# A graph transformer on one core: one token tile is attended without a rank, before the others

## Chip, cores, metric

One Trainium2 chip, one NeuronCore. The metric is the device time of one execution in microseconds (us). Engines are called PE (TensorE), DVE or VectorE, ACT (ScalarE), POOL (GpSimd) and SP (SyncE).

## The reference

Two layers of a graph transformer over N = 2708 tokens of width 512, with 8 heads of 64 and a hidden width of 2048, all in fp32. Each layer computes, with its own weights:

```python
mask = adj + eye(n)
q, k, v = (h @ W.T + b for W, b in ((Wq, bq), (Wk, bk), (Wv, bv)))     # 8 heads of 64
scores = where(mask == 0, -1e9, q k^T / 8)
ctx = softmax(scores) @ v
h1 = layer_norm(h + ctx @ Wo.T + bo)
h2 = layer_norm(h1 + relu(h1 @ W1.T + b1) @ W2.T + b2)
```

`adj` is a symmetric 2708 x 2708 integer matrix with about 9 ones in a row (at most 20), so a token attends to few others.

## The kernel before

Tokens are handled in tiles of 128; there are 22 tiles, and the last one, number 21, has 20 tokens.

**Lists.** While the keys and values of layer 0 are projected (22 tiles, `kv_d` in memory), each row of `adj` is read and VectorE takes from it the list of neighbours, up to 24 entries in `top` (`lists`). Then `counted` counts each row's neighbours and sums them by length. `ranked` turns that into a rank for each token, sorted by length with the longest first. It writes each token's record (its list and its own number) into the table `rec_d` at its rank, with 22 indirect DMAs from POOL, one for each tile, and loads the table back as `new`. From then on "tile g" means the 128 tokens with ranks 128 g and on. `listed` makes from `new` the gather indices `idx` and the mask terms `minus`; `ident_i` holds each rank's token.

**Slots.** `CAPS[g]` says how many neighbours the longest list of tile g may have: 22 for tile 0 down to 3 for tile 21, 210 in all. Attention of a tile gathers one key and value row for each token in each slot (`gather`, one indirect DMA of 128 rows of 4 KB for each slot), two slots to a chunk. For a chunk VectorE multiplies by the query (L1055) and reduces (L1061), ACT takes the exponentials (L1074) and weighs the second slot (L1081), VectorE weighs the first (L1087) and adds (L1094). At a tile's end `sums` and `divided` give its context `cx`. The first chunk may only be issued when `idx` of that tile exists; `kv` has five buffers.

**Order.** The kernel runs over 11 blocks of two tiles, in the order `blocks = [(20, 19), (18, 17), (7, 9), ...]`. In each block PE turns the two contexts (`flip`, L1191), projects them (`o`), VectorE normalises, and PE runs the feed-forward network in 16 steps f, `pf` (L1383) and `a` (L1356), with ACT's ReLU (`ft`, L1394) between them. Attention of later blocks is a generator; `advance(credit)` issues as many of its steps as the credit pays (a full chunk costs 1), and `through(k)` issues what block k still lacks, at f = 10 of the block before. At most two finished contexts wait at a time. The order of PE, ACT and SP is the program's; that of POOL and VectorE is too in the stage in question (`manual_schedule`), and elsewhere a scheduler sets it.

**Layer 0's queries.** After the keys come 22 queries (`first_queries`), tiles in order, from a second reading of x in blocks of 256 columns (`xg`), written to `q_d` at the tokens' own places. At t = 1 `ranked` is issued. At t = 12 (`OWN` − 1) the first lists are used. The first four rank tiles do not wait for `q_d`: their x rows are gathered (`own_rows`), turned and projected once more (`own_query`). Near the end of this stage block (20, 19) is attended and its contexts are projected.

**Layer 1** reuses ranks, lists and the same block order.

## Time and profile before

| | |
|---|---|
| median of 3 runs | 1948.09 us (1946.08 to 1949.13) |
| the profiled execution | 1944.02 us, span 1942.3 us |
| mean granted PE clock | 0.982 |
| keys of layer 0 | 0 to 157 us |
| queries of layer 0 and the first block's attention | 157 to 290 us |
| layer 0's blocks | 290 to 1145 us |
| change of layers | 1145 to 1235 us |
| layer 1's blocks | 1235 to 1942 us |

Engine times in the profile are busy times; a PE that is busy can still run at half the clock, which the granted clock shows. In a timeline, the bracket behind a row gives how long the engine stood idle before it and what released it. "Issue" means that no wait is seen.

### The profile page before, as it was taken

How to read it: one execution, taken by the hardware profiler on the slowest of the kernel's cores; microseconds unless marked ns; L12 is line 12 of the kernel's file. 1: busy time of each engine (PE TensorE's matmuls, PEld its weight loads, DVE VectorE, ACT ScalarE, POOL GpSimd, SP SyncE). 2: the span in 40 equal slices, each digit the busy share in tenths (PEclk: the TensorE clock that was granted, in tenths of full speed). 3: DMA queues.
4: the chain of work that ended last, by engine and by line, in shares of the span. 5: the costliest groups of instructions: out<-in, count | busy, mean ns of one | idle time of the engine just before them, and what ended most of it. 6: DMA issues, size and time to landing. Idle time of an engine off the chain costs nothing.

```text
span 1942.3 us, 20878 instructions
## 1 busy us (share of the span) xinstructions
PE 1859.4 (96%) x6162; PEld 1098.8 (57%) x6162; DVE 1321.4 (68%) x2172; ACT 934.0 (48%) x3219; POOL 804.6 (41%) x710
## 2 busy tenths in 40 slices
PE   8998968999999999999999997999999999999997
PEld 4443426556666565665666553566666665666664
DVE  5885467758658686785840337697977998878422
ACT  4560135545536555474452113556465766655511
POOL 3013525435536555463510114354555776546101
PEclk9999978999999999999999999999999999999999
DMA  9998747556645665554501368665665766544000
GB/s 330 345 319 297 260 151 269 181 176 198 199 159 181 215 201 175 188 185 151 170 17 65 110 237 325 215 220 186 216 213 165 262 215 235 184 154 151 17 1 19
DMA packets 131486, 366.92 MB, mean 189 GB/s; under 512 B 16669, under 2 KB 37005, under 8 KB 128655
## 3 DMA queue, kind: packets, MB, share of 16 engines
q0 software_dynamic: 69120, 246.35, 38.0%
q1 hardware_dynamic: 53332, 99.66, 14.9%
q10 hardware_dynamic: 8910, 19.48, 2.7%
q8 instruction: 50, 0.82, 0.2%
q14 instruction: 74, 0.60, 0.1%
HBM read 314.62 MB, written 50.83 MB: 188 GB/s over the span
## 4 chain that ended last, share of the span: by engine, by line
PE 48%; issue 3%; DVE 3%; DMA 1%; POOL 1%; ACT 1%; POOLq 0%; SPq 0%; DVEq 0%
PE pf L1383 19%; PE a L1356 18%; PE o L576 4%; PE q L576 2%; PE k L576 1%; PE v L576 1%; PE tp L1191 1%; DVE kv L1055 1%; POOL kv L1018 1%; DVE sc L1061 1%; DMA kv<-kv_d,idx 1%; PE a L1371 1%; DMA q<-q_d 0%; DVE acc L1094 0%; POOL rd L1181 0%
## 5 line engine op out<-in xcount | busy, mean ns | idle before, releaser
L1018 POOL DMA_INDIRECT kv<-kv_d,idx x420 | 544.5, 1296 | 461.8 <-DVE acc L1094 272.4
L1383 PE MATMUL pf<-hT,w 128*128 128x256 f32 (+1 forms) x2816 | 637.2, 374 | 6.7 <-ACT ft L1394 5.2
L1383 PEld LDWEIGHTS pf<-hT,w 128*128 128x128 f32 x2816 | 521.4, 192 | 181.8 <-issue 104.1
L1356 PE MATMUL a<-w,ft 128*128 128x512 f32 x1312 | 615.0, 595 | 6.1 <-ACT ft L1394 3.6
L1055 DVE TENSOR_TENSOR kv<-kv,q 128x1024 f32<-128x1024 f32 (+3 forms) x222 | 254.3, 1157 | 171.1 <-DMA kv<-kv_d,idx 139.9
L1394 ACT ACTIVATE ft<-pf,b 128x256 f32<-128x256 f32 (+1 forms) x336 | 153.8, 463 | 432.7 <-PE pf L1383 428.8
L1356 PEld LDWEIGHTS a<-w,ft 128*128 128x128 f32 x1312 | 247.8, 191 | 196.5 <-issue 169.3
L1081 ACT ACTIVATE kv<-kv,p 128x64 f32<-128x64 f32 x1232 | 311.0, 334 | 5.0
L1061 DVE TENSOR_REDUCE sc<-kv 128x16 f32<-128x1024 f32 (+3 forms) x222 | 253.7, 1152 | 1.5
L1094 DVE TENSOR_TENSOR acc<-acc,kv 128x1024 f32<-128x1024 f32 (+2 forms) x178 | 203.9, 1145 | 17.5 <-ACT kv L1081 15.5
L1181 POOL TENSOR_TENSOR rd<-va,mhalf 128x1 f32<-128x1 f32 (+1 forms) x88 | 90.0, 1023 | 273.5 <-DVE va L1179 271.9
L576 PE MATMUL o<-wo,cT 128*128 128x512 f32 x336 | 149.7, 598 | 0.5 <-ACT cT L1196 0.5
L1087 DVE TENSOR_TENSOR kv<-kv,p 128x512 f32<-128x512 f32 (+1 forms) x178 | 121.2, 681 | 36.1 <-ACT p L1074 36.1
L1074 ACT ACTIVATE p<-sc,minus 128x8 f32<-128x8 f32 x420 | 102.8, 294 | 72.0 <-DVE sc L1061 43.6
L1125 ACT ACTIVATE cx<-acc,su 128x64 f32<-128x64 f32 (+1 forms) x352 | 88.5, 334 | 71.1 <-DVE su L1117 54.2
L576 PEld LDWEIGHTS o<-wo,cT 128*128 128x128 f32 x336 | 64.1, 192 | 82.3 <-issue 72.1
L681 ACT ACTIVATE code<-aj 128x2708 bf16<-128x2708 int32 (+1 forms) x22 | 73.2, 3328 | 50.2 <-POOL aj L677 41.7
L684 DVE MAX8 tops<-code 128x8 f32<-128x247 f32 (+2 forms) x242 | 83.1, 401 | 20.1 <-ACT code L681 20.1
L1185 DVE SCALAR_TENSOR_TENSOR h<-h,rd,ln_b 128x512 f32<-128x512 f32 (+1 forms) x88 | 65.6, 746 | 41.1 <-POOL rd L1181 41.1
L1081 ACT ACTIVATE acc<-kv,p 128x64 f32<-128x64 f32 (+1 forms) x352 | 88.8, 335 | 1.4
L1443 ACT COPY kvs<-v 128x512 f32<-128x512 f32 (+1 forms) x22 | 12.9, 585 | 158.8 <-PE v L576 138.4
L1415 DVE TENSOR_TENSOR h<-a,h 128x512 f32<-128x512 f32 (+1 forms) x44 | 29.8, 678 | 83.3 <-PE a L1356 44.5
(159 smaller groups left out, 1586.8 us busy)
## 6 DMA issues: line engine op xcount, KB each, us to landing
aj<-in_adj SPq DMA_DIRECT2D x21, 1354.0 KB
kv_d<-kvs ACTq DMA_DIRECT2D x21, 512.0 KB
w<-in_W SPq DMA_DIRECT2D x20, 512.0 KB
xg<-in_xT SPq DMA_DIRECT2D x19, 512.0 KB
kv<-kv_d,idx POOLq DMA_INDIRECT x420
w<-in_W ACTq DMA_DIRECT2D x12, 512.0 KB
q_d<-qs SPq DMA_DIRECT2D x22, 256.0 KB
zT_d<-zT SPq DMA_DIRECT2D x22, 256.0 KB
```

The source lines that it names most:

```text
L576: nc.tensor.matmul(o[:r], xs(c), wm[:, c, :], start=(c == 0), stop=(c == NC - 1))
L1018: return nc.gpsimd.indirect_dma_start(out=to, out_offset=None, in_=table[:, :], in_offset=bass.IndirectOffsetOnAxis(ap=s, axis=0), bounds_ ...
L1055: nc.vector.tensor_tensor(kv[:r, :c, :DM], kv[:r, :c, :DM], self.q[:r].unsqueeze(1).to_broadcast([r, c, DM]), ALU.mult,)
L1061: nc.vector.tensor_reduce(self.sc[:r, s0 : s0 + c, :], kv[:r, :c, :DM].rearrange("p s (h d) -> p s h d", d=DK), AX.X, ALU.add,)
L1074: nc.scalar.activation(p[:r, s, :], self.sc[:r, s, :], AF.Exp, bias=minus[:r, g, s : s + 1])
L1081: nc.scalar.activation(to[:, i, hd], kv[:r, i, DM + h * DK : DM + (h + 1) * DK], AF.Copy, scale=p[:r, s0 + i, h : h + 1],)
L1087: nc.vector.tensor_tensor(to[:, 0, :].rearrange("p (h d) -> p h d", d=DK), kv[:r, 0, DM:].rearrange("p (h d) -> p h d", d=DK), p[:r, s0, : ...
L1094: nc.vector.tensor_tensor(self.acc[:r, :c, :], self.acc[:r, :c, :], kv[:r, :c, DM:], ALU.add)
L1181: nc.gpsimd.tensor_tensor(rd[:r], va[:r], mhalf[:r], ALU.pow)
L1356: nc.tensor.matmul(a[:r], fts[f][:, c0 : c0 + r], self.w2[f // 2][:, f % 2, :], start=(f == 0), stop=(f == NFC - 1),)
L1383: nc.tensor.matmul(pf[:, :w], self.w1[f // 2][:, c, f % 2 * P : f % 2 * P + P], hT[:, c, :w], start=(c == 0), stop=(c == NC - 1),)
L1394: nc.scalar.activation(ft[:, :w], pf[:, :w], AF.Relu, bias=self.b1[:, f : f + 1])
```

## The change

Tile 18 in token order (tokens 2304 to 2431, `STAR`) is taken out of the ranking. It keeps its tokens' own order and becomes place 20 (`FRESH`), with a cap of 18; the other tokens share the other places, and those whose rank falls behind place 20 move on by 128. The caps' sum becomes 221. In layer 0 place 20 is attended first, from indices made before the ranks are known. Its query is the first one computed, and it stays in SBUF. The order of tiles in both projections changes, so that the last x block read for the keys is the first used for the queries. The list tables leave their own pool for places of weight tiles that are not loaded yet. Own queries are left for one tile (19) instead of four. Layer 1 gets a block order of its own.

```diff
-CAPS = (22, 14, 13, 12, 12, 11, 11, 10, 10, 9, 9, 9, 9, 8, 8, 8, 7, 7, 7, 6, 5, 3)
+CAPS = (22, 14, 13, 12, 12, 11, 11, 10, 10, 9, 9, 9, 9, 8, 8, 8, 7, 7, 6, 5, 18, 3)
+FRESH, STAR = 20, 18
...
+        def carve(where, words, *shape):
+            if where not in room:
+                t = wts.tile([P, NC, XB], F32, tag=where, name="lists")
...
-        top = pa.tile([P, NT, LIST], F32, tag="top", name="top", bufs=1)
+        top = carve("w2_3", NT * LIST, LIST)
...
-        rec = pa.tile([P, NT, 32], F32, tag="rec", name="rec", bufs=1)
+        rec = carve("w1_3", NT * 32, 32)
...
+            nc.vector.memset(hot[:, STAR, :], 0.0)
+            yield
+            nc.gpsimd.tensor_copy(ident_i[:, FRESH : FRESH + 1], rec[:, STAR, LIST : LIST + 1])
+            listed_as(slice(FRESH, FRESH + 1), rec[:, STAR : STAR + 1, :LIST])
...
+            nc.vector.tensor_scalar(
+                over, places, FRESH * P - 0.5, float(P), ALU.is_gt, ALU.mult
+            )
+            nc.vector.tensor_tensor(ranks, places, over, ALU.add)
             moved = []
             for t in range(NT):
+                if t == STAR:
+                    continue
...
                 moved.append(move)
+                yield
...
+        stream = [XBS - 1] + list(range(XBS - 1))
+        stream += stream[:-1]
...
-        for t in range(NT):
+        for i, t in enumerate([NT - 2, NT - 1] + list(range(NT - 2))):
             r = size(t)
+            if i == NT - 2:
+                by_turns.enter_context(tc.manual_schedule(engines={mybir.EngineType.DVE}))
+                next(counts)
...
         nc.scalar.dma_start(**before)
+        counts = next(counts)
+        by_turns.close()
+        pa.__exit__(None, None, None)
+        at = ctx.enter_context(tc.tile_pool(name="at", bufs=2))
...
+        tiles = [STAR] + [t for b in range(STAR // 2, NT // 2) for t in (2 * b, 2 * b + 1)]
+        tiles = [t for i, t in enumerate(tiles) if i == 0 or t != STAR]
+        tiles += range(STAR // 2 * 2)
+        for j, t in enumerate(tiles):
             r = size(t)
+            q = project(tokens(t, 1), r, wq, "q", other=j % 2 > 0)
+            if j == 0:
+                to = new_q(FRESH)
+                nc.vector.scalar_tensor_tensor(to, q, DK**-0.5, bq, ALU.mult, ALU.add)
+                nc.sync.dma_start(out=q_d[0][t * P : (t + 1) * P, :], in_=to)
+                next(ahead)
...
+            if j == 2:
+                moving = ranked(*counts)
+                for _ in range(8):
+                    next(moving, None)
+            if j > 2:
+                advance(0.75)
+                if j < 10:
+                    next(moving, None)
+                    next(moving, None)
+                else:
+                    finish(moving)
+            if j == 11:
+                xr = own_rows(order[1])
+            if j == 18:
                 listed(True)
+                all_listed.append(True)
+                advance(1.5)
+            if j == 19:
                 listed(False)
+            if j == 20:
+                zT = turned_own(order[1], xr)
+                own_query(order[1], zT, new_q(order[1]), bq, wq)
+            meanwhile(j)
...
-    blocks = [(20, 19), (18, 17), (7, 9), (6, 10), (5, 11), (0, 16)]
+    blocks = [(FRESH, 19), (18, 17), (7, 9), (6, 10), (5, 11), (0, 16)]
     blocks += [(1, 15), (2, 14), (3, 13), (4, 12), (NT - 1, 8)]
+    plans = [blocks]
+    blocks = [(19, 18), (17, 16), (7, 9), (6, 10), (5, 11), (0, 15)]
+    blocks += [(FRESH, 14), (1, 13), (2, 12), (3, 4), (NT - 1, 8)]
+    plans.append(blocks)
...
-            if g == order[1]:
+            if g == order[1] or (n == 0 and g == order[0]):
                 steps += [None] * 3
+            if n == 0 and g == order[0]:
+                steps.append("more")
...
+            if step == "more":
+                while not all_listed:
+                    yield None
+                kv, begun = next(loaded), True
+                yield 1.0
+                continue
...
-        if len(now.w2) < 5:
+        if len(now.w2) < 3 or (j > 18 and len(now.w2) < 5):
             now.load_w1(len(now.w1), nc.scalar)
             now.load_w2(len(now.w2), nc.scalar)
...
+        if j == NT - 2:
+            advance(1.0)
+        if j == NT - 1:
             through(0)
+            early[0] = both(*(now.attended((g,), got) for g in blocks[0]))
```

`both` runs through the first tile's part (transposes, projection, norm), then the second's.

## The prediction

> **What bounds the kernel now.** I read the busy table first, then the forty slices, then stages by windows.
>
> ```profile
> PE 1859.4 (96%) x6162; PEld 1098.8 (57%) x6162; DVE 1321.4 (68%) x2172; ACT 934.0 (48%) x3219; POOL 804.6 (41%) x710
> ...
> PE   8998968999999999999999997999999999999997
> ...
> PEclk9999978999999999999999999999999999999999
> ```
>
> TensorE is busy 96% of the span; only slices 5 to 8 (about 195 to 435 us) show both digits down. The windows by stage put numbers on it; the columns are the stretch, its length, then busy time of PE, PEld, DVE, ACT and POOL with counts, granted clock, DMA share and GB/s.
>
> ```profile
> 25.00:157.00 132.00, 130.22 (x320) 56.96 (x318) 114.79 (x423) 77.10 (x40) 13.05 (x42) 1.00 0.95 337
> 157.00:290.00 133.00, 107.56 (x264) 48.71 (x264) 70.54 (x121) 25.78 (x96) 57.32 (x57) 0.90 0.67 231
> 290.00:430.00 140.00, 128.62 (x421) 80.44 (x422) 96.93 (x132) 73.49 (x280) 63.58 (x54) 0.95 0.62 213
> 430.00:1145.00 715.00, 704.58 (x2438) 429.22 (x2437) 452.29 (x651) 342.27 (x1262) 290.19 (x233) 1.00 0.50 163
> ```
>
> From 157 to 290 PE is idle 25 us and, at mean clock 0.90, its work is stretched besides. The PE timeline, then VectorE and GpSimd, say why (start, length, engine, line, operation; in brackets the idle time before and its releaser):
>
> ```profile
> 161.84 8.83 PE L576 MATMUL q<-wq,xg 128*128 128x512 f32 x16 [5.13 <-DVE kvs L879]
> 265.15 1.91 PE L1191 MATMUL tp<-ident,cx 128*128 128x128 f32 x4 [13.87 <-ACT cx L1125]
> 290.01 9.62 PE L1383 MATMUL pf<-hT,w 128*128 128x256 f32 x32 [0.46 <-ACT hT L1196]
> ...
> 223.70 1.23 DVE L1055 TENSOR_TENSOR kv<-kv,q 128x1024 f32<-128x1024 f32 x1
> ...
> 202.17 0.91 POOL L789 DMA_INDIRECT rec_d<-rec,ranks  x1 [0.30 <-issue]
> 207.74 0.19 POOL L819 CAST ident_i<-new 128x5 int32<-128x5 f32 x1 [0.32 <-DMA new<-rec_d]
> ```
>
> Attention cannot begin until the rank table is back (207.7 us), so its first multiply is at 223.7. VectorE, nearly idle from 162 to 212 (17 us busy in 50), then has eleven slots to do while TensorE runs out of queries: 13.9 us idle before the context transposes. Layer 0's first feed-forward starts at 290.0.
>
> **What the Trainium skill says.** "TensorE: Matmul & The Clock Gate", section "What's actually happening", says that about 3.4 us without work puts the array at half clock, and about 3.4 us of work frees it. The trace agrees: after the 13.9 us gap eight query matmuls take 5.71 us instead of 3.4. "VectorE: DVE Perf Modes", section "The perf-mode tier table", gives fp32 tensor_tensor and tensor_reduce the plain rate alone; here 1.16 and 1.15 us for 1,024 elements, so attention's VectorE price does not shrink. "DMA: Bandwidth & Descriptors", section "Issuing engines are not separate DMA queues", says that all issuers share the same 16 engines; 0.95 share in the keys stage agrees, so earlier gathers compete with weights and x blocks.
>
> **Prices, from rows of before.** One 128-token query: 3.44 us of PE. One own query (four transposes, copy, projection): 3.44 + 0.6. A full two-slot chunk on VectorE: 1.23 (L1055) + 1.22 (L1061) + 0.68 (L1087) + 1.22 (L1094) = 4.35 us; a first chunk has no L1094. A gather or a record move: 1.3 us per issue on POOL, and 4 to 7.5 us from issue to use under load (247.7 to 255.2).
>
> **Step 1, keys, 0 to 157: nothing.** The same tiles in another order, the 20-token tile second (2.1 us of PE). The DMA share of 0.95 sets the lists' pace, so VectorE ends them near 152.5 as before. The early x block has 148 columns, so tile 0 needs the next block at 16.6 us; it was issued at 7.3. Bound: 0 to +3; I take 0. The last block of x stays for tile 18's query, one load (0.5 MB) less.
>
> **Step 2, the start of queries: −5.** PE waited 5.13 us because the counting chain (152.8 to 161.2 on VectorE) and seven additions of the 20-token tile stood before the next evacuation. Now the chain is cut in two, both last key additions come between, and the small tile is long done. VectorE: first part to 155.1, additions to 156.5, the index of tile 18 to 156.8, the rest 6.1 us to 162.9. The three query banks let PE run on from 156.7.
>
> **Step 3, the fresh tile.** Its indices are ready at 157; the last key row is written at about 161; POOL issues eight gathers to 172, then 8 of 21 moves, then two moves with each query. Nine chunks, three in every four queries (credit 0.75): VectorE 38 us, beside evacuations of 0.69 us per query. That is 3 × 4.35 + 4 × 0.69 = 15.8 us in 13.8 us of PE, a lag of under 10 us, which six PSUM banks (20 us of queries) absorb. All of it lies in VectorE time that stood empty; the cover is the PE's query work to 237. POOL is now the tight queue: 18 gathers + 21 moves = 39 × 1.3 = 51 us, so moves end at 213 instead of 203, because moves stand behind gathers that wait for a key buffer. Lists are back at 217.5; they are used at j = 18, when PE is at 222 and VectorE, with DMA slips of 4 us, at about 228. So I charge 3 us for that.
>
> **Step 4, the first feed-forward: −23.** PE from 156.7: three queries 10.3, rank matmuls 2.4, small tile 1.05, seventeen queries 58.5, own query of tile 19 4.7, last query 3.4: 237. Three own queries are gone (12.1 us of PE). Tile 19 (five slots) runs on VectorE from its query at 234.5: 2.45 + 3.1 + 0.7 + 3.3 + 1.4 + 1.4 = 12.4, context 2 on ACT: 249; with the 3 us, 252. Meanwhile PE projects the fresh tile and then idles some 9 us, at half clock after. Transposes and copy 2, projection up to 5, norm 5.4 (278.6 to 284.1 before), turn 2: 267 against 290.0.
>
> **Step 5, block 0: −1.** Thirteen slots instead of fourteen remain for block 1, but none is begun (two chunks were, 8.7 us), and tile 18's query now comes by a gather behind the last norm's power on POOL, at about 263. Its key rows are loaded already. Up to the sums of tile 17 VectorE needs seven chunks, three steps of lag and two sums, about 35 us, with waits like before 5 and the context 2: 305. PE reaches the transposes unstalled at 267 + 36 = 303. Before, the same stretch took 47.8 us (290.0 to 337.8), so some 12 us were lost to ACT waiting on VectorE; now 3 to 20 may be. I take 11; bounds −9 and +8.
>
> **Step 6, other places.** Four weight tables (two pairs) are loaded at j = 19 and 20 instead of t = 1 and 2: 2.1 MB, 6 us of DMA beside tile 19's gathers, inside the 3 us charged. Their users come in block 0. Releasing the code pool earlier waits for lists that are done. From layer 0's block 2 on the slots are those of before: 0.
>
> **Step 7, layer 1: +5.** Caps sum to 221 instead of 210, so eleven gathers, five chunks (22 us of VectorE, 14 of ACT). Blocks 0 to 4 keep their slots. Block 5, (0, 15), has 30 for 29 and block 6, (20, 14), 26 for 22. The slack there is read from when contexts are ready and when PE turns them:
>
> ```profile
> 1480.00:1544.00 64.00, 64.00 (x227) 41.44 (x226) 59.04 (x81) 48.98 (x192) 44.74 (x33) 1.00 0.70 230
> 1544.00:1608.00 64.00, 64.00 (x227) 41.44 (x226) 60.70 (x81) 41.59 (x161) 46.69 (x30) 1.00 0.70 227
> ...
> 1539.38 2.01 ACT L1125 ACTIVATE cx<-acc,su 128x64 f32<-128x64 f32 x8
> 1542.17 2.17 ACT L1196 ACTIVATE cT<-tp,bv 128x128 f32<-128x128 f32 x8 [0.43 <-PE tp L1191]
> 1595.65 2.02 ACT L1125 ACTIVATE cx<-acc,su 128x64 f32<-128x64 f32 x8 [2.80 <-DVE su L1117]
> 1605.88 2.17 ACT L1196 ACTIVATE cT<-tp,bv 128x128 f32<-128x128 f32 x8 [1.68 <-PE tp L1191]
> ```
>
> VectorE is 92 to 95% busy; block 5 has no slack and block 6 has 7.5 us (1597.7 to the transposes at 1605.2). One slot more costs 1.6 us; two chunks 8.7 − 7.5 = 1.2; a half-clock window of 1.7 us for one or two of these: 5. Later blocks have 15 to 20 us and take 2 to 6.5. Bounds +2 and +12.
>
> **Sum.** −23 − 1 + 5 = −19. The profiled execution took 1944.02 us (span 1942.3, 1.7 around it), 4 us below the median 1948.09; so 1925 against it, and against the median 1929.
>
> **Rivals.** *POOL's order holds the ranks back (0.22).* If gathers wait 7 us a chunk, not 4.35, the moves stand behind them and the lists come 11 us later; tile 19 then sets the start at 278: 1940. For it: 4.4 and 9.4 us waits of POOL for buffers at 235 to 258. Against: five buffers, and no other tile competes. *Block 0 and POOL together take it all (0.06):* 11 us there, and 9 from block 0's worse bound: 1949; it needs both. *Slower (0.13): VectorE becomes layer 1's bound.* If the 22 us fall in blocks 5 and 6 with ReLU evacuations held behind attention on ACT (2.3 us of that stood at 1635 already), they reach PE with three half-clock windows (5) and that stall again (2): 29 − 24 gives +5: 1953. It decides once more than 24 us in layer 1 reach PE. Against it: two thirds of the added slots lie in blocks with slack. That the change does not do what it says is small: by the degrees of the given graph every cap suffices, so the fallback does not run.
>
> **Numbers.** Forecast 0.59 (1918 to 1935). A measurement of this kernel can tell about 0.2%, 4 us. Faster: 0.59 and nearly all of 0.22, so 0.80; the same 0.07; slower 0.13. Eight in ten reach from the best bounds (no slip in step 3, block 0 −9) near 1917 to the POOL rival's tail at 1945.
>
> **What would show it.** The first `pf` at 262 to 272, VectorE at least 35 us busy from 162 to 212, the last record move near 213, one PE gap of 6 to 12 us before tile 19's transposes; from first `pf` to layer 1's first `pf` 943 to 948 us (945.2 before); from there to the end 709 to 717 (707.1). A first `pf` after 280 makes the POOL rival right; over 725 in layer 1, the slower one.

## The result, and the profile after

The changed kernel takes **1960.27 us** (median of 5 runs, 1955.72 to 1967.44) against 1946.08 us for the kernel before, run beside it (1942.24 to 1949.13). The ratio is 1.0076, 95% interval 1.0049 to 1.0102: slower by 14 us, where 19 us less were forecast. The profiled execution has a span of 1957.3 us, 15.0 more than before.

The busy table and two of the rows in forty slices, of the kernel after:

```profile
PE 1849.3 (94%) x6126; PEld 1093.7 (56%) x6126; DVE 1364.0 (70%) x2215; ACT 959.0 (49%) x3334; POOL 833.2 (43%) x732
...
PE   8899847999999999999999997999999999999997
...
PEclk9999978999999999999999999999999999999999
```

TensorE is busy 10 us less than before (three own queries, 12 us by the forecast's price, are gone) in a longer span. The windows by stage (columns as before):

```profile
25.00:157.00 132.00, 125.88 (x294) 55.88 (x293) 113.75 (x416) 73.54 (x39) 13.18 (x43) 0.97 0.96 340
157.00:290.00 133.00, 100.84 (x241) 44.39 (x239) 92.03 (x146) 35.85 (x138) 74.54 (x66) 0.89 0.75 262
290.00:430.00 140.00, 119.59 (x398) 75.57 (x397) 87.41 (x122) 70.30 (x265) 57.99 (x51) 0.91 0.57 194
430.00:1145.00 715.00, 707.84 (x2455) 432.07 (x2453) 453.77 (x647) 349.19 (x1289) 296.26 (x238) 1.00 0.50 165
```

From 157 to 290 VectorE does 92 us instead of 71 and POOL 75 instead of 57: the empty time was filled. Yet PE, which has 7 us less to do there, is idle 32 us of the 133 instead of 25. Timelines of that stage follow; first PE:

```profile
163.89 10.46 PE L576 MATMUL q<-wq,xg 128*128 128x512 f32 x24
239.28 6.19 PE L576 MATMUL q<-wq,xg 128*128 128x512 f32 x8 [4.48 <-DVE qs L977]
253.55 0.60 PE L1241 MATMUL tp<-ident,cx 128*128 128x128 f32 x4
274.05 5.87 PE L576 MATMUL o<-wo,cT 128*128 128x512 f32 x8 [19.90 <-ACT cT L1246]
298.61 9.00 PE L1433 MATMUL pf<-hT,w 128*128 128x256 f32 x32 [0.46 <-ACT hT L1246]
```

Then POOL (the first gather, the first and the last record move, the reading back, the first lists), VectorE and ACT:

```profile
169.79 1.13 POOL L1065 DMA_INDIRECT kv<-kv_d,idx  x1 [22.44 <-DVE peak L1523]
180.40 2.08 POOL L809 DMA_INDIRECT rec_d<-lists  x1 [0.30 <-issue]
...
228.47 1.46 POOL L809 DMA_INDIRECT rec_d<-lists  x1 [0.30 <-issue]
234.56 0.86 POOL L823 DMA_DIRECT2D new<-rec_d  x1 [4.63 <-DMA rec_d<-lists]
237.30 0.20 POOL L842 CAST ident_i<-new 128x3 int32<-128x3 f32 x1
...
206.68 1.23 DVE L1101 TENSOR_TENSOR kv<-kv,q 128x1024 f32<-128x1024 f32 x1 [7.88 <-DMA kv<-kv_d,idx]
244.91 0.22 DVE L845 TENSOR_SCALAR idx<-new 128x72 int32<-128x72 f32 x1
257.04 1.23 DVE L1101 TENSOR_TENSOR kv<-kv,q 128x1024 f32<-128x1024 f32 x1 [6.03 <-DMA kv<-kv_d,idx]
281.65 0.68 DVE L1368 TENSOR_TENSOR h<-o,xb 128x512 f32<-128x512 f32 x1
292.56 0.69 DVE L1368 TENSOR_TENSOR h<-o,xb 128x512 f32<-128x512 f32 x1 [3.46 <-DMA xb<-in_x,ident_i]
...
271.73 2.02 ACT L1171 ACTIVATE cx<-acc,su 128x64 f32<-128x64 f32 x8 [5.81 <-DVE su L1163]
273.65 1.11 ACT L1246 ACTIVATE cT<-tp,bv 128x128 f32<-128x128 f32 x4
```

From 169.8 to 229.9 POOL issues its 18 gathers and 21 moves without a break: 0.30 us lie between one and the next throughout. The lists are back 30 us later than before (`ident_i`: 237.3 for 207.7) and 20 us later than forecast. VectorE turns them into gather indices only at 244.9, because that instruction stands in its order behind the fresh tile's last slots and three query evacuations. Tile 19's rows arrive 12 us after that. PE turned the fresh tile's context at 253.6, but the copy of it on ACT stands in program order behind tile 19's context: PE idles 19.9 us. The first `pf` starts at **298.6** instead of 290.0.

By stages: first `pf` +8.6; from it to layer 1's first `pf` (1241.63) 943.0 instead of 945.2, −2.2; from there to the end 715.7 instead of 707.1, +8.6. The sum is the 15.0 us.

Layer 1, the second window that the prediction showed, and two rows of ACT and one of PE:

```profile
1544.00:1608.00 64.00, 62.23 (x212) 39.89 (x211) 62.42 (x83) 44.28 (x175) 43.61 (x32) 0.97 0.70 234
...
1377.45 2.02 ACT L1171 ACTIVATE cx<-acc,su 128x64 f32<-128x64 f32 x8 [6.09 <-DVE su L1163]
1710.83 2.02 ACT L1171 ACTIVATE cx<-acc,su 128x64 f32<-128x64 f32 x8 [3.58 <-DVE su L1163]
...
1382.68 3.70 PE L1406 MATMUL a<-w,ft 128*128 128x512 f32 x8 [1.67 <-ACT ft L1444]
```

VectorE is 98% busy in the window where it was 95%, and PE loses 1.8 us and some clock (the same work starts 10 to 14 us later here than in before, so the two windows don't cover quite the same). In layer 1's second block ACT waits 6.09 us for a context's sums and the ReLU behind it is late: the block takes 74.1 us, before 70.8. In the seventh block (fresh tile, 14) it waits 3.58 us: 67.1 against 63.7. The last stretch is 1.6 us longer; the fifth block is 4.3 us longer and the sixth 4.2 us shorter.

### The profile page after: what moved, and what is told of

Read it like the earlier page. It is cut to its first block, busy times and chain, and to the rows that moved or that the text cites. A ratio compares the mean times of both kernels' runs of the same rounds, so it can differ in the third digit from the quotient of the medians.

```text
span 1957.3 us, 21027 instructions
## 1 busy us (share of the span) xinstructions
PE 1849.3 (94%) x6126; PEld 1093.7 (56%) x6126; DVE 1364.0 (70%) x2215; ACT 959.0 (49%) x3334; POOL 833.2 (43%) x732
## 5 line engine op out<-in xcount | busy, mean ns | idle before, releaser
L1065 POOL DMA_INDIRECT kv<-kv_d,idx x442 | 567.9, 1285 | 477.4 <-DVE acc L1140 248.4
L1101 DVE TENSOR_TENSOR kv<-kv,q 128x1024 f32<-128x1024 f32 (+1 forms) x232 | 268.1, 1165 | 218.8 <-DMA kv<-kv_d,idx 182.6
L1127 ACT ACTIVATE kv<-kv,p 128x64 f32<-128x64 f32 x1328 | 335.3, 335 | 5.4
L1107 DVE TENSOR_REDUCE sc<-kv 128x16 f32<-128x1024 f32 (+1 forms) x232 | 267.5, 1161 | 2.0
L1140 DVE TENSOR_TENSOR acc<-acc,kv 128x1024 f32<-128x1024 f32 (+2 forms) x188 | 217.2, 1155 | 18.8 <-ACT kv L1127 16.0
L1231 POOL TENSOR_TENSOR rd<-va,mhalf 128x1 f32<-128x1 f32 (+1 forms) x88 | 94.1, 1069 | 283.1 <-DVE va L1229 282.1
L576 PE MATMUL o<-wo,cT 128*128 128x512 f32 x336 | 153.2, 609 | 20.8 <-ACT cT L1246 20.8
L1120 ACT ACTIVATE p<-sc,minus 128x8 f32<-128x8 f32 (+1 forms) x442 | 108.0, 293 | 113.5 <-DVE sc L1107 113.5
L1133 DVE TENSOR_TENSOR kv<-kv,p 128x512 f32<-128x512 f32 (+1 forms) x188 | 127.9, 681 | 20.7 <-ACT p L1120 20.7
L1171 ACT ACTIVATE cx<-acc,su 128x64 f32<-128x64 f32 (+1 forms) x352 | 88.6, 334 | 79.4 <-DVE su L1163 58.5
L576 PE MATMUL k<-wk,xg 128*128 128x512 f32 x168 | 80.2, 623 | 11.1 <-DVE kvs L914 6.1
L1028 POOL DMA_INDIRECT kv_d<-kvs,ident_i x22 | 23.2, 1056 | 157.6 <-ACT kvs L1493 92.0
```

Of the source, the lines that this page charges most:

```text
L576: nc.tensor.matmul(o[:r], xs(c), wm[:, c, :], start=(c == 0), stop=(c == NC - 1))
L1065: return nc.gpsimd.indirect_dma_start(out=to, out_offset=None, in_=table[:, :], in_offset=bass.IndirectOffsetOnAxis(ap=s, axis=0), bounds_ ...
L1101: nc.vector.tensor_tensor(kv[:r, :c, :DM], kv[:r, :c, :DM], self.q[:r].unsqueeze(1).to_broadcast([r, c, DM]), ALU.mult,)
L1107: nc.vector.tensor_reduce(self.sc[:r, s0 : s0 + c, :], kv[:r, :c, :DM].rearrange("p s (h d) -> p s h d", d=DK), AX.X, ALU.add,)
L1120: nc.scalar.activation(p[:r, s, :], self.sc[:r, s, :], AF.Exp, bias=minus[:r, g, s : s + 1])
L1127: nc.scalar.activation(to[:, i, hd], kv[:r, i, DM + h * DK : DM + (h + 1) * DK], AF.Copy, scale=p[:r, s0 + i, h : h + 1],)
```

## Experiments

All are edits of the kernel after unless said otherwise. The table has, for each: median and ratio to the kernel before beside it (95% interval), then from the profile the time at which VectorE makes tile 19's indices, the first `pf`, the time between these two, layer 1's first `pf`, and the time from there to the end.

| run | us | ratio | indices | first pf | between | layer 1 | its length |
|---|---|---|---|---|---|---|---|
| before | 1946.08 | | | 290.0 | | 1235.2 | 707.1 |
| after | 1960.27 | 1.0076 (1.0049–1.0102) | 244.9 | 298.6 | 53.7 | 1241.6 | 715.7 |
| e1_turn | 1957.53 | 1.0072 (1.0048–1.0095) | 246.8 | 296.1 | 49.3 | 1240.1 | 715.5 |
| e2_latew | 1959.91 | 1.0084 (1.0056–1.0112) | 243.3 | 293.5 | 50.2 | 1240.1 | 714.2 |
| e3_lead | 1960.27 | 1.0077 (1.0052–1.0103) | 240.1 | 294.1 | 54.0 | 1239.7 | 719.5 |
| e4_fresh6 | 1946.12 | one run | 230.2 | 284.1 | 53.9 | 1226.5 | 717.6 |
| e5_l1cap7 | 1957.29 | 1.0053 (1.0037–1.0068) | 246.3 | 300.9 | 54.6 | 1246.3 | 711.0 |
| e6_dveorder | 1952.06 | 1.0023 (1.0012–1.0035) | 245.9 | 292.0 | 46.1 | 1234.1 | 718.2 |
| e7_ranks | 1975.55 | 1.0148 (1.0123–1.0172) | 227.9 | 310.1 | 82.2 | 1255.1 | 720.2 |
| e8_all | 1956.07 | 1.0059 (1.0036–1.0081) | 226.8 | 296.9 | 70.2 | 1236.1 | 714.0 |
| e9_before_order | 1943.52 | 0.9991 (0.9981–1.0002) | | 290.1 | | 1233.8 | 709.2 |
| e10_best | 1948.17 | 1.0013 (1.0003–1.0024) | 239.3 | 282.3 | 43.0 | 1225.8 | 721.1 |
| e11_rows | 1958.40 | 1.0065 (1.0039–1.0091) | 237.1 | 291.5 | 54.4 | 1233.4 | 722.2 |
| e12_l1order | 1958.43 | 1.0064 (1.0045–1.0083) | 243.9 | 297.7 | 53.9 | 1239.3 | 709.9 |
| e13_best_l1 | 1941.98 | 0.9996 (0.9984–1.0008) | 240.2 | 283.3 | 43.2 | 1231.8 | 713.6 |
| e14_no_latew | 1941.42 | 0.9990 (0.9981–0.9999) | 236.8 | 282.5 | 45.7 | 1222.2 | 713.1 |
| e15_l1cap7 | 1945.57 | 1.0016 (1.0008–1.0025) | 237.2 | 280.1 | 42.9 | 1224.8 | 718.1 |

Single executions of one kernel differ by up to some 8 us from its median; the columns from the profiles are of one execution each. The indices move by some 3 us between profiles whose edits lie behind them. The time from the indices to the first `pf` is steadier: 53.7 to 54.6 us in the six profiles of after's own arrangement (after, e3, e4, e5, e11, e12). So it is the better measure of an edit behind the indices.

### What makes the first feed-forward late

**Less of the fresh tile (e4_fresh6): 6 slots in layer 0, its other 12 gathers and their slots left out.**

```diff
+FEW = {(0, 20): 6}      # slots of the fresh tile in layer 0
...
```

> In layer 0 the fresh tile attends to its first 6 neighbours alone; 12 gathers and 6 chunks are left out. Theory (POOL's queue): gathers and record moves share one queue at 1.4 to 1.5 us each, so the lists come 12 x 1.45 = 17 us earlier, at 218 to 222 instead of 237.3, tile 19's rows with them, and the first pf at 279 to 284, since PE reaches tile 19's own query at about 243 anyway. Rival (VectorE is the bound in this stage): 6 chunks of 4.35 us = 26 us less work there make the same difference, but then VectorE shows no wait for key rows before; with the queue theory those waits (7.9, 3.5, 3.2 us) are what goes, and VectorE's busy time from 180 to 245 falls by no more than the left-out chunks.

POOL's last move and the lists:

```profile
208.15 0.92 POOL L810 DMA_INDIRECT rec_d<-lists  x1 [0.30 <-issue]
219.78 0.19 POOL L843 CAST ident_i<-new 128x3 int32<-128x3 f32 x1 [4.42 <-DMA new<-rec_d]
```

The lists are back 17.5 us earlier, as the theory said. The indices gain only 14.7 us: they are made at 230.2, where they stand among the queries (`j == 18`), and no longer wait for the table. The first `pf` comes at 284.1, 14.5 earlier, layer 1's first `pf` 15.2 earlier, and the span is 13.2 shorter. So the twelve slots are the price; the run does not say whether as POOL's issues or as VectorE's work. The next one does.

**The gathers without the work (e11_rows): all 18 gathers issued, six slots multiplied.**

```diff
+FEW = {(0, 20): 6}
...
+            if (n, g) == (0, FRESH):
+                steps += ["rows"] * 6      # take two gathered rows, multiply nothing
```

> The kernel after, where in layer 0 all 18 gathers of the fresh tile are issued but only its first six slots are multiplied (its output is then not the attention over all neighbours). Theory (GpSimd's queue and the DMA traffic set the lists' return): lists back at 232 to 238 as in after, first pf 292 to 299, the whole 1954 to 1960. Rival (VectorE's twelve slots are the cost): lists back 218 to 224 and first pf 284 to 288, as with six slots in all, the whole 1945 to 1948.

The last move, reading back and lists on POOL, a weight load on ACT, and the indices on VectorE, then windows of this run (busy times of PE, PEld, DVE, ACT and POOL, granted clock, DMA share, GB/s), and after them those of after:

```profile
225.34 0.94 POOL L810 DMA_INDIRECT rec_d<-lists  x1 [0.31 <-issue]
231.13 0.86 POOL L824 DMA_DIRECT2D new<-rec_d  x1 [4.85 <-DMA rec_d<-lists]
237.13 0.18 POOL L843 CAST ident_i<-new 128x3 int32<-128x3 f32 x1 [3.26 <-DMA new<-rec_d]
...
230.91 0.37 ACTq L1272 DMA_DIRECT2D w<-in_W  x1
...
237.09 0.23 DVE L846 TENSOR_SCALAR idx<-new 128x72 int32<-128x72 f32 x1 [5.64 <-DMA new<-rec_d]
...
162.00:245.00 83.00, 78.42 (x192) 34.98 (x191) 39.57 (x86) 10.72 (x40) 51.49 (x49) 0.97 0.88 295
198.00:226.30 28.30, 28.30 (x68) 12.52 (x67) 5.79 (x12) 2.02 (x8) 21.87 (x22) 1.00 0.86 284
```

```profile
162.00:245.00 83.00, 76.51 (x181) 33.38 (x180) 60.92 (x100) 24.91 (x99) 53.20 (x44) 0.96 0.74 247
180.00:230.00 50.00, 49.09 (x114) 21.23 (x112) 37.42 (x41) 18.99 (x76) 40.48 (x32) 1.00 0.77 255
```

VectorE had 21 us less to do and waited idle for the table; the lists were back at 237.1, as in after (237.3). With 6 gathers they were back at 219.8. So **the twelve gathers, in POOL's queue and on the DMA engines, hold the lists back**, even where nothing is multiplied.

That the two times agree to 0.2 us is luck. POOL's last move ended at 226.3, 3.7 us earlier than in after, though its first gather had begun 1.9 us later: its 39 operations took 54.6 us, not 60.1. Then a pair of weight tables was issued just ahead of the reading back, which took 6.0 us at a DMA share of 1.02 (231.1 to 237.1) and in after 2.7 us at 0.10 (234.6 to 237.3). So **VectorE's slots lengthen POOL's queue**, by 5.5 us here. In after 15 of the 39 operations took 1.4 us or more, with VectorE 75% busy from 180 to 230. In e11 6 did, all before 198, while the six slots were worked; of the 21 after that, with VectorE 20% busy, none took over 1.04 us, although the DMA share was higher (0.86 for 0.77). In e7_ranks below the moves from 204 to 215, beside an idle VectorE, took 0.92 to 0.98 us. Why an issue takes longer beside VectorE's work no run here shows.

The other cost of VectorE's slots is the 7.6 us between the table and its indices in after (237.3 to 244.9; here none). The indices came 7.8 us earlier than in after, and in e4 another 6.9; behind them all three take about the same time. So e4's 14.5 us split in two halves, VectorE's slots and the gathers. The expectation had named one cause; both count. The timed median moved by only 1.9 us, since layer 1 took 722.2 in this run.

**Ranks ahead of the gathers (e7_ranks): all 21 moves after five chunks' gathers, lists and own query earlier.**

```diff
             if j == 2:
                 moving = ranked(*counts)
-                for _ in range(8):
+                for _ in range(NT - 1):
                     next(moving, None)
...
-            if j == 18:
+            if j == 10:
                 listed(True)
...
-            if j == 20:
+            if j == 16:
                 zT = turned_own(order[1], xr)
...
-            if len(ready) > EARLY:
+            if len(ready) > (4 if n == 0 and g == order[0] else EARLY):
```

> All 21 record moves are issued at j = 2, after the gathers of five chunks (one more than before) and ahead of the other four; the lists are used at j = 10 instead of 18, and tile 19's own query is made at j = 16. Theory (the order of POOL's queue and the place where lists are used): moves end near 212 instead of 230, the table is back near 221, tile 19's rows are issued right behind the fresh tile's last chunk, by about 232 instead of 246, and tile 19's context is ready at 254 to 260 instead of 273.7; the first pf comes at 276 to 285. The whole is 8 to 18 us shorter than the changed kernel. Rival (POOL's total work alone): 18 gathers and 21 moves take the same time in any order, so tile 19's rows come no earlier than 240 and the first pf after 292.

Worse by 11.5 us at the first `pf`. POOL, VectorE and PE:

```profile
214.50 0.92 POOL L809 DMA_INDIRECT rec_d<-lists  x1 [0.30 <-issue]
226.27 1.15 POOL L842 CAST ident_i<-new 128x3 int32<-128x3 f32 x1 [2.85 <-DMA new<-rec_d]
...
222.97 1.22 DVE L1096 TENSOR_TENSOR kv<-kv,q 128x1024 f32<-128x1024 f32 x1 [19.30 <-DMA kv<-kv_d,idx]
...
228.03 6.25 PE L576 MATMUL q<-wq,xg 128*128 128x512 f32 x8 [9.70 <-DVE qs L977]
253.68 5.38 PE L576 MATMUL q<-wq,zT 128*128 128x512 f32 x8 [10.79 <-ACT zT L1238]
```

The moves end 14 us sooner and the lists 11 us sooner, but the gathers behind them are late instead: VectorE stands 19.3 us in front of a multiply, with query evacuations queued behind it, so PE runs dry. Tile 19's own query, which stood at 246.6 on PE in after, comes at 253.7. What stands second in POOL's queue is late, and the fresh tile's rows cost more there than the moves did.

**The fresh tile turned before tile 19 is attended (e1_turn).**

```diff
         if j == NT - 2:
             advance(1.0)
+            parts.extend(now.attended((g,), got) for g in blocks[0])
+            next(parts[0])
         if j == NT - 1:
             through(0)
-            early[0] = both(*(now.attended((g,), got) for g in blocks[0]))
+            early[0] = both(*parts)
```

> The fresh tile's context is turned (PE transposes and the ACT copy into cT, and the load of its x rows) right after tile 19's own query, before any of tile 19's attention steps; its projection follows at its old place. Theory (ACT's order): the 19.9 us in which PE stands before the fresh tile's projection are a copy on ACT that sits behind tile 19's exponentials, weighing and context. Then the projection runs at about 255 instead of 274, tile 19's x rows are loaded earlier, and the first pf comes near 287 (286 to 290) instead of 298.6; the whole is 9 to 12 us shorter. Rival (the lists alone): tile 19's context at 273.7 sets everything; the first pf stays within 3 us of 298.6.

The projection moved into the gap (255.1), but the first `pf` moved by 2.5 us only, the rival's number. In this run the indices came 1.9 us later; from them to `pf` it took 49.3 us instead of 53.7, so ACT's order was worth 4.4 us and not the 19.9 of PE's gap. VectorE put five chunks of tiles 17 and 18 among the two norms, and the second norm's result ended at 294.4. Removing one thing that stood in front of the norm only showed the next.

**VectorE in program order in block 0 (e6_dveorder: e1_turn, and this).**

```diff
-            in_order.enter_context(tc.manual_schedule(engines={mybir.EngineType.Pool}))
+            in_order.enter_context(
+                tc.manual_schedule(engines={mybir.EngineType.Pool, mybir.EngineType.DVE})
+            )
```

> The fresh tile's context is turned early, as in e1_turn, and VectorE keeps the program's order in layer 0's block 0 too, so none of tile 18's and 17's multiplications can stand before tile 19's sums and norm. Theory (interleaved attention): in e1_turn 14 us of those multiplications stood among the two norms, and tile 19's norm ended 10 us after its projection; now 5.5 us after it, and the first pf comes at 284 to 288 instead of 296. As this work is only moved, block 0 is 4 to 8 us longer, and the whole gains 0 to 4 us. Rival (the x rows of tile 19, behind the first norm's power on POOL, set the norm): the first pf stays after 292.

First `pf` 292.0, not the theory's 284 to 288 and at the rival's edge: the second norm still waits 3.44 us for tile 19's x rows. It is 4.1 us before e1_turn although the indices were hardly earlier: from indices to `pf` 46.1 us, 3.2 less than there. Block 0 took 76.6 us (82.4 in after), so it gave nothing back. Of the edits tried alone or in a pair, only this pair has a ratio clearly below that of after (1.0012 to 1.0035 against 1.0049 to 1.0102).

**The same order in the kernel before (e9_before_order).** The diff is that of e6_dveorder's second part, in the kernel before.

> The kernel before, with VectorE in program order in layer 0's block 0. In it two chunks of tile 18 (4.9 us of VectorE) ran ahead of the last norm at 273 to 278. Theory (attention steps put ahead of norms by the scheduler cost time, whatever the order of tiles): the first pf at about 285 to 287 instead of 290.0 and the whole 2 to 6 us shorter, ratio 0.997 to 0.999. Rival (the chunks only move and block 0 pays them back): first pf 3 to 5 us earlier, layer 1's first pf within 1.5 us of 1235.2, ratio 1.000.

First `pf` 290.1, where theory and rival both had it 3 to 5 us earlier: neither. Layer 1's first `pf` (1233.8) and the ratio 0.9991 (0.9981 to 1.0002) are those of the rival. Two chunks of tile 18 still stand ahead of the norm there, at 273 to 278 us, so they do by program order too. The edit hardly changed what stands in front of the norm in the kernel before, and so says little about a free order in general.

**Two weight pairs loaded in block 0 (e2_latew).**

```diff
-        if len(now.w2) < 3 or (j > 18 and len(now.w2) < 5):
+        if len(now.w2) < 3:
```

> The two pairs of weight tables loaded at j = 19 and 20 are loaded in block 0 instead (f = 0 and 2). Theory (shared DMA engines): the DMA share of 1.01 from 252 to 275 delays tile 19's key rows, 11 us from issue to use; without 2.1 MB beside them they come 3 to 6 us earlier and the first pf moves from 298.6 to 293 to 296; block 0 may lose 0 to 2 us. Rival (the list's lateness alone): the rows arrive no more than 1 us earlier and the first pf stays within 1.5 us.

Tile 19's first multiply came 8.7 us after its indices instead of 12.1, as the theory said. First `pf` 5.1 us earlier, 1.6 of it from earlier indices, but layer 1's first `pf` only 1.6 us: block 0 took 85.7 us for 82.4, where 0 to 2 us of loss were expected, with a stall of 10.40 us for a ReLU (9.30 in after). e14_no_latew below undoes this edit in a better neighbourhood.

**The keys stage (e3_lead): VectorE starts each list a little later.**

```diff
-            while done < min(NT, 1 + LEAD * i):
+            while done < min(NT, 1 + LEAD * max(0.0, i - 0.7)):
```

> The lists are issued 0.7 of a tile later against the keys (1 + 1.3 (i - 0.7)). Theory: with the 20-token tile second the lists run 4.8 us ahead of PE's key tiles, and on VectorE one key addition fell behind a whole list; the 6.1 us gap of PE at 65 and the half clock after it (1.7 to 3.4) go, and the queries begin at 156 to 158 instead of 163.9. The first pf comes 4 to 8 us earlier, 291 to 295. Rival: VectorE's scheduler puts another list before another key addition, a gap of 4 us or more stays between 25 and 160, and the queries begin after 161.

In after and then in this run, the one wait of PE in that stage:

```profile
65.14 6.22 PE L576 MATMUL k<-wk,xg 128*128 128x512 f32 x8 [6.12 <-DVE kvs L914]
```

```profile
62.72 3.70 PE L576 MATMUL k<-wk,xg 128*128 128x512 f32 x8 [3.34 <-DVE kvs L914]
```

A key addition stands behind a whole list on VectorE. The gap got 2.8 us shorter, the queries began at 159.0 and the first `pf` came 4.5 us earlier. The six profiles with this edit have the first query at 155.2 to 159.0, the nine without it at 162.3 to 165.8. Layer 1 was 3.8 us longer in this run and the timed runs show nothing.

**Everything at once with early ranks (e8_all: e7, e6, e2 and e3).**

> e7_ranks, e6_dveorder, e2_latew and e3_lead together. If their causes add: lists 4 us earlier from the keys, tile 19's norm 8 us earlier, the rows 3 us earlier, so the first pf at 262 to 272, and the whole at 1932 to 1946, at or under the kernel before. If instead VectorE's own work up to block 1 is the bound (fresh tile, 19, 18, 17 and three chunks of 7: about 126 us with evacuations and norms, from 170 on), what the first pf gains comes back as a wait of PE for ACT in block 0: block 0 takes over 88 us (82 in the changed kernel), and the whole stays over 1950.

Missed: 296.9. The early ranks spoil the rest, although the indices stood ready at 226.8. Block 0 took 78.6 us, not over 88, so VectorE's own work as the bound did not show either.

**Without the early ranks (e10_best: e1, e2, e3 and the order of e6).**

> The kernel after with four of the earlier edits together: the fresh tile's first step before tile 19's attention, VectorE in program order in block 0, weight pairs 3 and 4 in block 0, and VectorE's lead in the keys stage as in the earlier run. Theory (each removed a delay of its own on the way to the first feed-forward): first pf at 281 to 286, layer 1's first pf at 1225 to 1230, the whole 1944 to 1949, ratio 0.998 to 1.001. Rival (one limit, the late return of the ranks, stands behind all of them): first pf 289 to 292, the whole 1950 to 1953.

First `pf` 282.3 and layer 1's first `pf` 1225.8, as the theory said, 9.4 us before the kernel before. From the indices it took 43.0 us to the first `pf`, 10.7 less than in after. One by one the edits had given 4.4 (e1, ACT's order), 3.5 (e2, the weights) and 3.2 (e6 over e1, VectorE's order): 11.1 in all, so these causes about add up. But layer 1 took 721.1 us in that run, so the sum is no gain: 1.0013.

### What makes layer 1 longer

**Seven slots for the fresh tile there (e5_l1cap7), longer lists cut off.**

```diff
+FEW = {(1, 20): 7}      # slots of the fresh tile in layer 1
...
```

> In layer 1 the fresh tile attends to its first 7 neighbours alone, as tiles 16 and 17 do; 11 gathers and their 5 chunks in layer 1 are left out, layer 0 is that of the changed kernel. Theory (slots): from layer 1's first pf to the end the changed kernel took 715.7 us and the kernel before 707.1; without the eleven slots it takes 706 to 710, and the whole is 6 to 10 us shorter than the changed kernel (1951 to 1954). Rival (layer 1's own block order or the scheduler's placing of VectorE's work costs the time, whatever the slots): it stays at 713 or more.

Layer 1 took 711.0 us, 4.7 less than in after, between theory and rival; the median, 1957.29, misses the theory's 1951 to 1954. The blocks tell more than the sum. The fourth to the seventh, which hold tile 0 and the fresh tile, take 257.5 us with seven slots; with 18 they take 262.7 in after, and 260.9 to 263.5 in the ten profiles of this order. So the eleven slots cost some 5 us there. What stays lies in the second block (75.9 us, in after 74.1, before 70.8), which does not hold the fresh tile.

**Another block order in layer 1 (e12_l1order).**

```diff
-    blocks = [(19, 18), (17, 16), (7, 9), (6, 10), (5, 11), (0, 15)]
-    blocks += [(FRESH, 14), (1, 13), (2, 12), (3, 4), (NT - 1, 8)]
+    blocks = [(19, 18), (17, 16), (7, 9), (FRESH, 15), (6, 10), (5, 11)]
+    blocks += [(0, 14), (1, 13), (2, 12), (3, 4), (NT - 1, 8)]
```

> The kernel after, with another block order in layer 1: (19,18), (17,16), (7,9), (20,15), (6,10), (5,11), (0,14), (1,13), (2,12), (3,4), (21,8). The fresh tile's 18 slots stand four blocks earlier, away from tile 0's 22. Theory (in after the fresh tile's slots crowd behind tile 0's, where VectorE is 92 to 95% busy): from layer 1's first pf to the end 709 to 712 instead of 715.7, the whole 1953 to 1957. Rival (the eleven added slots cost the same wherever they stand): 714 to 718, the whole 1958 to 1962.

The profiled execution, the fastest of seven, agrees (709.9, second block 70.6), the timed runs say 1958.4, the rival's number; as a whole inconclusive. The fourth to the seventh block, which hold the same tiles as in after, take 257.6 us, as with seven slots. With the four edits of e10_best it was run again:

**e13_best_l1 (e10_best and this order), and e14_no_latew (the same without e2_latew's edit).**

> The kernel after with the four edits that brought layer 1's first pf to 1225.8, and layer 1's other block order as well. Theory (in layer 1 the fresh tile's 18 slots behind tile 0's 22 are what costs): first pf 280 to 286, layer 1's first pf 1224 to 1230, from there to the end 709 to 713 instead of 721.1, the whole 1935 to 1942, ratio 0.995 to 0.998, shorter than both kernels. Rival (layer 1 takes back whatever comes early, whatever its order): 717 to 722 in layer 1, the whole 1943 to 1948.

> As the run with all five edits, but weight pairs 3 and 4 are loaded at j = 19 and 20 as in after. Theory (loading them in block 0 only moves the traffic): first pf 3 to 6 us later, 285 to 290, block 0 3 to 5 us shorter, layer 1's first pf within 2 us of the run with five edits. Rival (the loads delay the start and nothing gives it back): layer 1's first pf 4 to 6 us later.

Layer 1: 713.6 and 713.1 us instead of 721.1, a little above what was expected of the order, and medians of 1941.98 and 1941.42. The fourth to the seventh block take 257.6 us in both, 5.2 less than in e10_best. The first stage of e13 is as expected (283.3), its layer 1 begins 2 us later than that (1231.8). PE in e14_no_latew, from tile 19's context on:

```profile
266.35 1.91 PE L1241 MATMUL tp<-ident,cx 128*128 128x128 f32 x4 [17.68 <-ACT cx L1171]
268.72 5.43 PE L576 MATMUL o<-wo,cT 128*128 128x512 f32 x8 [0.46 <-ACT cT L1246]
280.93 1.11 PE L1241 MATMUL tp<-ident,h 128*128 128x128 f32 x4 [6.34 <-DVE h L1235]
282.50 8.83 PE L1433 MATMUL pf<-hT,w 128*128 128x256 f32 x32 [0.46 <-ACT hT L1246]
```

From the context's transposes to `pf` it now takes 16.2 us, in after 24.6 from the fresh tile's projection at 274.1, which waited for the same context. The late weight loads were no gain: without them the way from the indices to `pf` was 2.5 us longer, but block 0 was 4.9 us shorter (76.4 for 81.3). The profile has layer 1's first `pf` 9.7 us earlier, but 3.4 of that were there at the indices already. The timed medians differ by 0.6 us: e13's profiled execution (1947.17) was the slowest of its 14, e14's (1937.16) one of the fastest. Against the kernel before e13 has 0.9996 (0.9984 to 1.0008), not the forecast gain; e14 has 0.9990 (0.9981 to 0.9999): at most 0.2% better, which is within what a measurement can tell from no change. Its profiled execution is 7.0 us shorter than that of before, more than its median shows.

**Seven slots in the new order (e15_l1cap7).**

> As the run with all five edits, but in layer 1 the fresh tile attends seven slots instead of 18 (longer neighbour lists are cut off there). Theory (in the new order the added slots lie in slack): layer 1 within 2 us of the run with five edits. Rival (added slots cost wherever they stand): layer 1 4 to 8 us shorter, 703 to 707.

Neither: 718.1 us, longer with fewer slots. But the fourth to the seventh block take 257.5 us, with 18 slots 257.6: where the added slots stand, the theory holds, and in this order they cost nothing. The excess lies in the second block again, 80.0 us, with ACT waiting 8.76 us for a context's sums.

Over all runs with the block order of after the second block of layer 1 took from 72.6 to 79.7 us; the slots in it are those of the kernel before (70.8), and VectorE's operations there come in the same order in before, after and e10_best. ACT's wait in front of the context, `<-DVE su`, follows: 2.79 us before, 6.09 in after, and in e10_best

```profile
1365.01 2.02 ACT L1171 ACTIVATE cx<-acc,su 128x64 f32<-128x64 f32 x8 [7.23 <-DVE su L1163]
```

Late rows look like the cause in after, where VectorE waits 6.04 us for gathered rows at 1360.2 and 4.11 at that place before. They don't explain the runs, though: e9_before_order waits 6.08 us there with a second block of 72.6 us, e10_best 5.83 with 79.2. In e12, e13 and e14 that context falls into the third block; the second takes 70.6 to 72.5, the third 71.1 to 72.7 instead of 68.4. In e15 it falls into the second again. What makes the second block of layer 1 so unlike from run to run no run here shows; it stays open.

## Why the prediction was wrong

**The step that failed is step 4**, "the first feed-forward: −23", with the lists' return that it took from step 3. It put the first `pf` at 267; it came at 298.6. The 31.6 us divide at two marks: tile 19's indices, forecast for 228, came at 244.9 (+17); from there to its context in PE's reach it took 29 us (244.9 to 273.7) instead of 24 (228 to 252), +5; from the context to `pf` 25 instead of 15, +10.

**The indices (+17).** They were sized in steps 2 and 3. Queries began at 163.9, not 156.7: PE's wait of 6.12 us in the keys stage and 2.6 us for the slow matmuls after it, where step 1 had bounded the loss at +3. The last key rows went out at 164.7, and the gathers, which by the kernel's own dependency wait for them, began at 169.8 instead of about 161 (+9). (The row of the first gather names `peak`; but in all fifteen profiles with this tile it follows the last key rows by 5.1 to 6.5 us, whatever is named.) POOL's 39 operations took 60 us, not 52 (+8): an issue took 1.0 to 2.1 us, 1.5 with the pause after it, not 1.3. From the last move's end to the table it took 7.4 us instead of 4.5 (+3). Only VectorE took its turn sooner, 7.6 us after the table, where 10.5 had been forecast (−3).

The POOL rival had the right queue and the wrong mechanism. Its mark, "a first pf after 280", was met, but it let gathers "wait 7 us a chunk" for key buffers, and POOL waited for no buffer. The term that was mis-sized is the price of an operation: 1.3 us came from rows of before in which VectorE was nearly idle, and e11_rows shows that the very work moved there made the operations longer. e4_fresh6 and e11_rows together show that the gathers, more than the slots, set the lists' return. The rival was priced at 11 us, the step charged 3, and the lists came back 20 us late.

**Tile 19's rows (+5).** Step 4 counted from its query. In the run the gathers decided: 12.1 us from indices to the first multiply (244.9 to 257.0), with the DMA at a share of 1.01 from 252 to 275 us, where the four weight tables of step 6 and tile 18's rows land too. That is what the Trainium skill says in "DMA: Bandwidth & Descriptors", section "Issuing engines are not separate DMA queues": the weights, issued by ACT and not by POOL, compete all the same. The runs agree: "Inside the 3 us charged" was wrong, for with the weights moved away (e2_latew) the rows were there 8.7 us after the indices, 3.4 us sooner, though block 0 took it back.

**From the context on (+10).** The words "Meanwhile PE projects the fresh tile" failed. The step followed PE's order and not ACT's: the copy of the fresh tile's context is issued after tile 19's context, and ACT works in program order. Then five chunks of tiles 17 and 18 ran on VectorE before and among the first norm, and the second norm waited 3.46 us for an x row tile gathered after the first norm's power on POOL. Of the 53.7 us from the indices to `pf`, 39 were forecast. ACT's order was worth 4.4 (e1_turn), the weights 3.5 (e2_latew), VectorE's order 3.2 (e6_dveorder over e1_turn); e10_best, with all three, took 43.0. The 4 us that are left are about the wait for the x rows, 3.43 us in that run too; no run takes that wait away, so this last part is argued.

**What held.** VectorE's work did go into time that had stood empty (35.6 us busy from 162 to 212, at least 35 forecast), though not for nothing: it lengthened POOL's issues and held up the indices. From first `pf` to layer 1's first `pf` 943 to 948 was forecast: 943.0. That was luck in part: step 5's "−1" for block 0 was +5.1 (82.4 for 77.3), and block 1 returned 3.5, later places 3.8. Layer 1's +5 was +8.6, within its bounds; the eleven slots cost some 5 us in the fourth to the seventh block, so that term was right. Most of the rest is the second block's 3.3 us, which the prediction did not have. One reading of the slices was loose and changed nothing: both digits are down only in the sixth and seventh slice (243 to 340 us), not from 195 to 435.

**The slower rival** expected a loss in layer 1 of more than 24 us. That was not it: layer 1 stayed inside the forecast's own bounds. The kernel became slower because the first part's gain did not exist: step 4 is off by 31.6 us of the 34 by which the profiled execution misses the forecast, layer 1 by 3.6, and the stretch between gave 1.2 back.

## What to carry to other kernels

When work is moved into an engine's empty time, price the queue that feeds it: here VectorE had the room, and 18 gathers on the queue that also carried 21 record moves delayed a table that everything later waited for. And take that queue's price from a stretch as busy as the new one will be: 39 operations took 60.1 us beside VectorE's slots and 54.6 us with twelve of these left out. Where a step is said to run "meanwhile", follow it through each engine's program order to its last copy; one copy behind another tile's context left PE idle for 19.9 us and put 4.4 us on the way to the feed-forward. And take the chain after the late event as long as it is when little covers it: from tile 19's indices to the feed-forward PE was busy 58.5 of 79.1 us in the kernel before, and 20.8 of 53.7 us in the changed one.

## What was not expected of the hardware

- An indirect DMA occupied POOL for 0.91 to 1.13 us in most cases, but for 1.4 to 2.1 us in 15 of 39 cases in after (the pause of 0.30 us not counted). The long ones came while VectorE worked: none of the 22 moves in the kernel before (VectorE 21% busy from 175 to 203, DMA share 0.69), none in e11_rows after 198 (20%, share 0.86), but 11 of 21 moves in after (75% from 180 to 230, share 0.77). So the DMA share does not explain them.
- In the keys stage a single wait of 6.12 us also slowed what came next: eight matmuls took 6.22 us instead of 3.60 (granted clock 0.60 from 65 to 71.5 us).
- Reading the table of ranks back took 2.7 us in after at a DMA share of 0.10, and 6.0 us in e11_rows at 1.02, when two weight tables had been issued by ACT just ahead of it.
- Layer 1's first block took 70.7 to 71.0 us in all profiles, its second 70.6 to 80.0.
